# Segment attention with batch norm on one core: batch statistics inside the last attention arm, five output groups loaded into attention's space, output groups in pairs on the two row halves of TensorE

## The chip, the core and the metric

The kernel runs on one NeuronCore of a Trainium2 chip. A core has five engines with an instruction stream each: TensorE (PE, matmuls), VectorE (DVE), ScalarE (ACT), GpSimd (POOL) and SyncE (SP). PE reads SBUF and writes PSUM. DMAs are issued by SP, ACT and POOL, each through a queue of its own, and all share the core's 16 DMA engines. The metric is the device time of one execution in microseconds; the median of 9 runs of the kernel before is 382.57 us (381.2 to 386.01).

## What is computed

`feat` holds 16384 rows of 256 numbers, `bids` a segment number from 0 to 7 for each row. Rows are placed into 8 padded segments of at most 3072 rows, attention runs inside each segment, the result goes through `Wt`, a batch norm over all 16384 rows follows, and its positive part is added to `feat`:

```
q = feat @ Wq; k = feat @ Wk; v = feat @ Wv
starts = jnp.searchsorted(bids, jnp.arange(B, dtype=bids.dtype))
pos = jnp.arange(N, dtype=bids.dtype) - starts[bids]
...
attn = jax.nn.softmax(jnp.where(mask[:, None, :], scores, NEG), axis=-1)
rp = jnp.einsum('blm,bmd->bld', attn, vp)
r = rp[bids, pos]
t = r @ Wt
mu = t.mean(axis=0); var = t.var(axis=0)
tn = (t - mu) / jnp.sqrt(var + EPS) * gamma + beta
return feat + jax.nn.relu(tn)
```

The `bids` of the input are not sorted, so the starts come out as 0, 1441, 1441, 3121, 3677, 3677, 15838 and 15838, and most rows fall outside the padded window of their segment. About 430 to 730 rows per segment have a place of their own ("list" rows); 199 more read a place that another row owns; all others read a row at one end of their segment ("edge" rows, 16 different values in all).

## The kernel before

**Attention.** For each segment `b` a list of at most 6 tiles of 128 rows is gathered by POOL (`gather`, line 821). `project(b)` transposes the tiles on PE (line 904), copies them to `xT` and makes queries, keys (`qs[b % 2]`, `ks[b % 2]`) and values (`vs[b % 2]`, line 938). `scores` (line 948) makes score tiles and ACT's exponentials write them to `pr_a` and `pr_b` (line 953). `sums` (line 983) multiplies them with the values (line 989), divides (lines 993, 994) and leaves the tile in `tk`; `moment` adds it and its square to `acc` (lines 974 to 979). The number of tiles per segment (4, 5 or 6) is known only on the chip, so four segments form one arm of a `tc.Switch` with 81 arms; here the segments take 4, 4, 5, 6 and 6, 6, 4, 4 tiles. Each finished segment is written to `t_rows` in DRAM by SP (line 1005). In the last segment (`b == NB - 1`) POOL gathers the 16 edge rows into `E` (line 1018); `late` and `e_late` add those that lie in the last segment (line 1000); lines 1029 and 1030 finish `E`. Line 1032 takes a square root of a constant on ACT, meant to bring in the square root's table; nothing ties it to this place.

**Between.** Lines 1338 to 1348 check that all denominators are in range and leave a count in `bad`. Then the pools of attention are closed (`att.close()`), and `io` (6 buffers `f` of 1 MB), `fin` and the PSUM pools of the output stage take their space. Lines 1369 to 1388 sum `acc` and `E` over partitions with two matmuls of 512 columns, and make mean, variance, root, `scale` and `shift`; lines 1392 to 1403 turn `E` into the normalised edge rows `y3`, split in three bf16 parts on 48 partitions of each row half of PE.

**Output.** `feat` and `out` are handled as 16 groups of 1024 rows, in the list `ORDER` (0 to 6, 15 to 12, 7 to 11). SP loads a group into one of the 6 buffers (line 1427); for each pair of its 8 row tiles, PE selects the edge rows with the one-hot tile `hot` (line 1435, 48 rows, 256 columns, bf16), and DVE adds the result to the group (line 1446). In four of the steps a second group is taken along, whose `feat` is added on PE through the identity (line 1440, f32) and brought back by ACT (line 1444). ACT issues the group's store (line 1448). Between the groups, `normal` runs the list rows in `tk` through three DVE operations per two tiles (lines 1409, 1412, 1415).

**Scatter.** POOL writes the 48 tiles of `tk` and 3 of `L` to their rows of `out` with one indirect DMA each (`put`, line 1463). The stores of groups and these writes hit the same tensor, so a tile of segment `b` waits until the groups that hold its rows have landed. `waits` gives the number of groups in the order of `ORDER`: for this input 3 for segment 0, 5 for segments 1 and 2, 7 for 3 to 5, 11 for 6 and 7, and all 16 for `L`. The order on DVE and PE after attention is chosen by the scheduler; only the start of the kernel stands in a block with a written order (`tc.manual_schedule`).

Of the kernel before, what the change touches and what calls it, by code (L numbers as in the profile page):

```python
# [9 lines left out]
F32 = mybir.dt.float32  # L10
I32 = mybir.dt.int32
BF16 = mybir.dt.bfloat16
# [6 lines left out]
P = 128  # L19
# [512 lines left out]
def segment_attention_bn_kernel(  # L532
# [43 lines left out]
    with ExitStack() as short:  # L576
# [52 lines left out]
        root = fs.tile([P, 1], F32, name="root")  # L629

# [5 lines left out]
        vs = [fw.tile([P, FT, D + 1], F32, name=f"vs{i}", bufs=1) for i in range(2)]  # L636
        xT = fw.tile([P, DH, FW], F32, name="xT", bufs=1)


        qs = [fw.tile([P, FW], F32, name=f"q{i}", bufs=1) for i in range(2)]  # L640
        ks = [fw.tile([P, 2, P], F32, name=f"k{i}", bufs=1) for i in range(2)]

        pr_a = fw.tile([P, FT, QA], F32, name="pr_a", bufs=1)
        pr_b = fw.tile([P, FT, FW - QA], F32, name="pr_b", bufs=1)
# [338 lines left out]
        def sums(b, u, T, e_late):  # L983
# [13 lines left out]
            if b % PART == PART - 1:  # L997
                moment(at)
            if e_late is not None:
                nc.tensor.matmul(  # L1000
                    e_late, late[:, u, :], tk[:, at, :], start=(u == 0), stop=(u == T - 1)
                )
            if u == TMIN - 1 or u == T - 1:
                u0, u1 = 0 if u < TMIN else TMIN, FT if u == T - 1 else TMIN
                nc.sync.dma_start(
                    t_rows[b * FW + u0 * P : b * FW + u1 * P, :].rearrange(
                        "(t p) d -> p t d", p=P
                    ),
                    tk[:, b * FT + u0 : b * FT + u1, :],
                )  # L1010

        def attend(b, T):
# [15 lines left out]
            if b == NB - 1:  # L1028
                nc.vector.tensor_add(E[:, 0, :], E[:, 0, :], e_late)
                nc.vector.tensor_mul(E[:, 1, :], E[:, 0, :], E[:, 0, :])  # L1030

                nc.scalar.activation(root, eps_t, AF.Sqrt)
# [121 lines left out]
        def edge_selection():  # L1154


            C = N // 2 // (GT * P)
            for c in range(C):
                eb = hotp.tile([P, GT * P], BF16, tag="eb", name=f"eb{c}", bufs=2)
                nc.vector.memset(eb, 99.0)  # L1160
                for r in range(2):
                    nc.sync.dma_start(
                        eb[64 * r : 64 * r + 3 * NE, :],
                        edge_of[ts(r * C + c, GT * P)].unsqueeze(0).to_broadcast(
# [140 lines left out]
        for a in range(NB // PART):  # L1305
# [31 lines left out]

        lim = fw.tile([P, TT], F32, tag="lim", name="lim", bufs=1)
        nc.vector.tensor_scalar(lim, rdens, LIM, None, ALU.is_lt)
        good = fw.tile([P, TT], F32, tag="good", name="good", bufs=1)  # L1340
        odd = fw.tile([P, 1], F32, tag="odd", name="odd", bufs=1)
        nc.vector.scalar_tensor_tensor(
            good, rdens, 1.0 / LIM, lim, ALU.is_gt, ALU.mult, accum_out=odd
        )
        nc.vector.tensor_scalar(odd, odd, -1.0, float(TT), ALU.mult, ALU.add)
        ps_bad = ps_a.tile([P, 1], F32, tag="px", name="ps_bad")
        nc.tensor.matmul(ps_bad, ones, odd, start=True, stop=True)
        nc.vector.tensor_tensor(bad, ps_bad, over, ALU.add)
        att.close()


        fin = short.enter_context(tc.tile_pool(name="fin", bufs=1))
        io = short.enter_context(tc.tile_pool(name="io", bufs=IOB))
        psM = short.enter_context(tc.tile_pool(name="psM", bufs=1, space=PSUM))
        psY = short.enter_context(tc.tile_pool(name="psY", bufs=2, space=PSUM))
        psF = short.enter_context(tc.tile_pool(name="psF", bufs=4, space=PSUM))
        feat3 = feat.rearrange("(g p i) d -> g p i d", p=P, i=GT)
# [11 lines left out]
        sums = psM.tile([P, 2, D], F32, name="sums")  # L1369
        nc.tensor.matmul(sums, ones, acc, start=True, stop=False)  # L1370
        nc.tensor.matmul(sums, wE, E[0:NE, :, :], start=False, stop=True)
        mom = fin.tile([P, 2, D], F32, name="mom")
        nc.vector.tensor_scalar(mom, sums, 1.0 / N, None, ALU.mult)
        mean, var = mom[:, 0, :], mom[:, 1, :]
        sq_m = fin.tile([P, D], F32, name="sq_m")
        nc.vector.tensor_mul(sq_m, mean, mean)
        nc.vector.tensor_sub(var, var, sq_m)
        nc.vector.tensor_scalar(var, var, 0.0, None, ALU.max)
        root_v = fin.tile([P, D], F32, name="root_v")
        nc.scalar.activation(root_v, var, AF.Sqrt, bias=eps_t)  # L1380
        nc.vector.reciprocal(root_v, root_v)
# [4 lines left out]
        nc.vector.tensor_mul(scale[:, 0, :], root_v, gamma_bc)  # L1386
        nc.vector.tensor_mul(shift[:, 0, :], mean, scale[:, 0, :])
        nc.vector.tensor_sub(shift[:, 0, :], beta_bc, shift[:, 0, :])

        yE = fin.tile([P, D], F32, name="yE")
        nc.vector.tensor_mul(yE, E[:, 0, :], scale[:, 0, :])
        nc.vector.tensor_add(yE, yE, shift[:, 0, :])
        nc.vector.tensor_scalar(yE, yE, 0.0, None, ALU.max)
        for s in range(2):
            yh = fin.tile([P, D], BF16, name=f"yh{s}")
            nc.vector.tensor_copy(yh, yE)
            yh_f = fin.tile([P, D], F32, name=f"yhf{s}")
            nc.vector.tensor_scalar(yh_f, yh, later_part[:, s : s + 1], None, ALU.mult)  # L1400
            nc.vector.tensor_sub(yE, yE, yh_f)
        y3 = fin.tile([P, D], BF16, name="y3")
        nc.vector.tensor_copy(y3, yE)  # L1403
        tc.no_sync_barrier()

        def normal(y, x, t, T):

            py = psY.tile([P, 2, D], F32, tag="py", name="py")
            nc.vector.tensor_tensor(
                py[:, 0:T, :], t, scale.to_broadcast([P, T, D]), ALU.mult  # L1410
            )
            nc.vector.tensor_tensor(
                py[:, 0:T, :], py[:, 0:T, :], shift.to_broadcast([P, T, D]), ALU.add
            )
            nc.vector.scalar_tensor_tensor(y, py[:, 0:T, :], 0.0, x, ALU.max, ALU.add)
# [5 lines left out]
        units = iter(range(0, TT, 2))  # L1421
        steps = [(0,), (1,), (2,), (3, 4), (5,), (6, 7), (8,), (9, 10), (11,), (12, 13)]
        for step in [*steps, (14,), (15,)]:
            held = {}
            for k in step:
                held[k] = io.tile([P, GT, D], F32, tag="f", name=f"f{ORDER[k]}")
                nc.sync.dma_start(held[k], feat3[ORDER[k]])
            for i in range(0, GT, 2):
                for k in step:
                    g = ORDER[k]  # L1430
                    r = slice(64 * (g // (NG // 2)), 64 * (g // (NG // 2)) + 3 * NE)
                    pf = psF.tile([P, 2, D], F32, tag="pf", name=f"pf{g}")
                    two, on_pe = held[k][:, i : i + 2, :], k != step[0]
                    for u in range(2):
                        nc.tensor.matmul(  # L1435
                            pf[:, u, :], hot[r, g % (NG // 2), i + u, :], y3[r, :],
                            start=True, stop=not on_pe,
                        )
                        if on_pe:
                            nc.tensor.matmul(  # L1440
                                pf[:, u, :], ident, two[:, u, :], start=False, stop=True
                            )
                    if on_pe:
                        nc.scalar.copy(two, pf)  # L1444
                    else:
                        nc.vector.tensor_add(two, two, pf)  # L1446
            for k in step:
                dense.append(nc.scalar.dma_start(out3[ORDER[k]], held[k]).ins)
# [83 lines left out]
```

## Time and profile before

| what | value |
|---|---|
| median of 9 runs | 382.57 us |
| the profiled execution's own time | 385.01 us |
| its span, first to last instruction | 382.9 us |
| last operation of the last tile in attention (line 1030) | ends at 255.56 us |
| first group load issued | 258.09 us |
| `y3` ready (line 1403) | 273.12 us |
| first store of a group issued | 280.32 us |
| first scatter | 296.25 us |
| last scatter starts | 371.34 us |

Busy shares over the whole span are 75% for PE, 69% for DVE, 45% for POOL and 28% for ACT, but they are averages over very different stages: PE is near full in attention (64.14 of the 66 us from 174 to 240), the DMA engines are nearly idle there (a share of 0.16) and full in the output stage. An entry "L1435 PE MATMUL" means the instruction that line 1435 issued on PE; "PEld" is PE's weight load; "SPq" and "ACTq" are instructions that issue a DMA; the part in brackets is the engine's idle time just before, with what ended it.

### The profile page before, as it was taken

How to read it: one execution, taken by the hardware profiler on the slowest of the kernel's cores; microseconds unless marked ns; L12 is line 12 of the kernel's file. 1: busy time of each engine (PE TensorE's matmuls, PEld its weight loads, DVE VectorE, ACT ScalarE, POOL GpSimd, SP SyncE). 2: the span in 40 equal slices, each digit the busy share in tenths (PEclk: the TensorE clock that was granted, in tenths of full speed). 3: DMA queues.
4: the chain of work that ended last, by engine and by line, in shares of the span. 5: the costliest groups of instructions: out<-in, count | busy, mean ns of one | idle time of the engine just before them, and what ended most of it. 6: DMA issues, size and time to landing. Idle time of an engine off the chain costs nothing. (4 is left out here: it accounts for less than half of the span.)

```text
span 382.9 us, 4089 instructions
## 1 busy us (share of the span) xinstructions
PE 287.3 (75%) x1103; PEld 178.3 (47%) x1103; DVE 263.9 (69%) x789; ACT 105.9 (28%) x199; POOL 173.8 (45%) x180
## 2 busy tenths in 40 slices
PE   1348839879899999599989999953179899897000
PEld 0224626548486578238765777640134443343000
DVE  8988459997959546447992464663996649678930
ACT  8810432222631352354322533411001021111000
POOL 3258377878856766600483000103000537775760
PEclk9999988998999999859999999985555555555555
DMA  4011002031402202111240020239869999999820
GB/s 115 13 34 55 10 8 63 15 113 38 143 19 84 74 22 94 53 43 41 77 139 1 0 85 0 83 103 335 347 239 370 380 373 387 387 417 402 332 81 2
DMA packets 21485, 53.38 MB, mean 139 GB/s; under 512 B 6606, under 2 KB 14112, under 8 KB 17322
## 3 DMA queue, kind: packets, MB, share of 16 engines
q1 hardware_dynamic: 12277, 25.85, 19.5%
q10 hardware_dynamic: 2421, 16.83, 10.6%
q0 software_dynamic: 6720, 10.02, 8.4%
q14 instruction: 51, 0.42, 0.4%
q8 instruction: 16, 0.26, 0.3%
HBM read 26.67 MB, written 29.92 MB: 148 GB/s over the span
## 5 line engine op out<-in xcount | busy, mean ns | idle before, releaser
L821 POOL DMA_INDIRECT xs<-in_r_feat,idx x48 | 58.8, 1225 | 61.0 <-DVE upto L871 43.1
L989 PE MATMUL po<-vs,pr_a 128*128 128x257 f32 x312 | 77.2, 391 | 4.5 <-ACT pr_a L953 2.9
L1463 POOL DMA_INDIRECT out<-tk,idx x48 | 47.3, 985 | 57.9 <-DMA f<-in_r_feat 33.0
L989 PEld LDWEIGHTS po<-vs,pr_a 128*128 128x128 f32 x312 | 57.3, 193 | 18.5 <-ACT pr_a L953 5.0
L821 POOL DMA_INDIRECT reads_r<-reads_of,idx x48 | 51.2, 1067 | 21.7 <-issue 12.5
L1435 PE MATMUL pf<-y,hot 48*128 48x256 bf16 x128 | 36.5, 399 | 22.3 <-DVE y L1403 11.1
L1446 DVE TENSOR_TENSOR f<-f,pf 128x512 f32<-128x512 f32 x48 | 30.9, 686 | 18.3 <-PE pf L1435 18.2
L934 PE MATMUL pv<-wvt,xT 128*128 128x256 f32 x164 | 39.2, 393 | 0.0
L1435 PEld LDWEIGHTS <-hot 48*128 48x128 bf16 x128 | 14.2, 122 | 51.9 <-issue 48.2
L1440 PE MATMUL pf<-f,ident 128*128 128x256 f32 x64 | 37.9, 706 | 0.0
L934 PEld LDWEIGHTS pv<-wvt,xT 128*128 128x128 f32 x164 | 31.9, 198 | 9.1 <-ACT q L926 2.0
L948 PE MATMUL s<-q,k 32*128 32x512 f32 (+2 forms) x124 | 31.8, 566 | 3.0 <-DVE q L925 3.0
L978 ACT ACTIVATE sq<-tk 128x256 f32<-128x256 f32 x39 | 16.3, 417 | 62.7 <-DVE tk L994 51.7
L1444 ACT COPY f<-pf 128x512 f32<-128x512 f32 x16 | 9.4, 586 | 73.7 <-PE pf L1440 73.7
L904 PE MATMUL px<-ident,xs 128*128 128x128 f32 x82 | 17.6, 329 | 15.8 <-DVE xT L908 5.6
L953 ACT ACTIVATE pr_a<-s,mask 128x512 f32<-128x512 f32 x39 | 24.1, 687 | 18.1 <-PE s L948 17.9
L915 PE MATMUL pqk<-xT,wqk 128*128 128x512 f32 (+2 forms) x52 | 25.1, 629 | 0.3 <-DVE xT L908 0.3
L904 PEld LDWEIGHTS px<-ident,xs 128*128 128x128 f32 x82 | 10.3, 160 | 28.4 <-issue 13.0
L1440 PEld LDWEIGHTS pf<-f,ident 128*128 128x128 f32 x64 | 16.5, 312 | 11.2 <-issue 10.7
L993 DVE RECIPROCAL rdens<-po 128x1 f32<-128x1 f32 x39 | 6.3, 163 | 21.7 <-PE po L989 21.6
L938 ACT COPY vs<-pv 128x512 f32<-128x512 f32 (+1 forms) x21 | 12.1, 577 | 30.4 <-PE pv L934 30.4
L821 POOL DMA_INDIRECT E<-t_rows,eidx x1 | 1.1, 1074 | 42.8 <-issue 42.8
(241 smaller groups left out, 414.3 us busy)
## 6 DMA issues: line engine op xcount, KB each, us to landing
f<-in_r_feat SPq DMA_DIRECT2D x16, 1024.0 KB, 8.6
out<-f ACTq DMA_DIRECT2D x16, 1024.0 KB, 8.8
t_rows<-tk SPq DMA_DIRECT2D x4, 768.0 KB, 3.9
t_rows<-tk SPq DMA_DIRECT2D x4, 512.0 KB, 3.2
eb<-edge_of SPq DMA_DIRECT2D x16, 96.0 KB, 2.4
t_rows<-tk SPq DMA_DIRECT2D x4, 256.0 KB, 2.4
xs<-in_r_feat,idx POOLq DMA_INDIRECT x48, 2.8
reads_r<-reads_of,idx POOLq DMA_INDIRECT x48, 2.5
```

What stands on the lines that cost most here:

```text
L821: nc.gpsimd.indirect_dma_start(out=dst, out_offset=None, in_=table, in_offset=bass.IndirectOffsetOnAxis(ap=ind, axis=0), bounds_check=n - ...
L904: nc.tensor.transpose(px[:, ts(t, P)], xs[:, b * FT + t0 + t, ts(h, P)], ident)
L915: nc.tensor.matmul(pqk[:, 0:w], wqk[:, h, :], xT[:, h, own_c], start=(h == 0), stop=(h == DH - 1),)
L934: nc.tensor.matmul(pv[:, t, :], xT[:, h, ts(t0 + t, P)], wvt[:, h, :], start=(h == 0), stop=(h == DH - 1),)
L948: nc.tensor.matmul(s[:, i, 0:w], k[g, t // 4, :], q[g, c : c + w], start=True, stop=True)
L953: nc.scalar.activation((pr_b if c else pr_a)[:, t, 0:w], s[:, i, 0:w], AF.Exp, bias=mask[:, m : m + 1],)
L978: nc.scalar.activation(sq, tk[:, at, :], AF.Square)
L989: nc.tensor.matmul(po, pr[:, t, ts(r, P)], v[:, t, :], start=(t == 0), stop=(t == T - 1))
L1435: nc.tensor.matmul(pf[:, u, :], hot[r, g % (NG // 2), i + u, :], y3[r, :], start=True, stop=not on_pe,)
L1440: nc.tensor.matmul(pf[:, u, :], ident, two[:, u, :], start=False, stop=True)
L1446: nc.vector.tensor_add(two, two, pf)
L1463: w = nc.gpsimd.indirect_dma_start(out=out, out_offset=bass.IndirectOffsetOnAxis(ap=idx[:, at : at + 1], axis=0), in_=y, in_offset=None, b ...
```

## The change

The diff below leaves out comments, the parts that only move, and the last arm's unchanged lines.

- `xT`, `qs`, `ks`, `vs`, `pr_a` and `pr_b` become slices of one tile `work` that lives as long as the kernel's main part. Five group buffers (`f_bufs`) are other views of the same space; a sixth is made in `io` after attention. Buffer 0 covers `xT` and part of the even queries, buffer 1 the rest of the queries, the keys and part of the even values, buffers 2 to 4 the rest, with all of `pr_a` and most of `pr_b`.
- At the end of the last segment's `attend`, SP issues the loads of the first five groups, and `statistics()` makes mean, root, `scale_s` and `y3` there, on tiles that exist already (`late` as scratch). In the instruction order of the arm that this input takes, SP issues the load of buffer 0 before the store of segment 6 to `t_rows`, and the other four after it.
- Line 1032's square root is replaced by one on the denominator of the last tile but one, so it cannot run earlier. In the instruction order this removes two table loads from the arm's first segment and puts one between the squares of the last segment's tiles.
- The store of the last segment to `t_rows` goes from SP to POOL.
- Groups go in pairs of consecutive entries of `ORDER`. Each pair has an even and an odd group, and `hot` keeps even groups in one row half and odd ones in the other, so PE gets alternating halves. Pairs 0 and 1 add both groups on DVE; pairs 2 to 7 add the even entry on DVE and the odd one on PE and ACT. Operations of the list rows follow each add: none in pairs 0 and 1, 4 in pairs 2 and 3, then 3. The order on DVE and PE is the written one.
- `short_path_holds` (the check of the denominators) comes after pair 3. `scale` and `shift` are made after pair 1.
- `L` waits for the largest count among the segments (11 here) instead of 16. The bound of the scatter's index check is put in a register once.

```
+        wide = DH * FW + 2 * FW + 4 * P + 2 * FT * (D + 1) + FT * FW
+        work = fs.tile([P, wide], F32, name="work")
...
+        parts = [work[:, c : c + n] for c, n in zip(begins, sizes)]
+        xT = parts[0].rearrange("p (h c) -> p h c", h=DH)
+        qs = parts[1:3]
...
+        f_bufs = [
+            work[:, c : c + GT * D].rearrange("p (i d) -> p i d", i=GT)
+            for c in range(0, sum(sizes) - GT * D + 1, GT * D)
+        ]
...
+            if b == NB - 1 and u == T - 2:
+                nc.scalar.activation(root, rdens[:, one], AF.Sqrt)
...
+                dma = nc.sync if b < NB - 1 else nc.gpsimd
+                dma.dma_start(
...
+        def statistics():
+            free = late.rearrange("p t m -> p (t m)")
+            msq, var, yE = (free[:, ts(i, D)] for i in range(3))
+            s1 = ps_o.tile([P, D], F32, tag="po", name="s1")
+            s2 = ps_o.tile([P, D], F32, tag="po", name="s2")
+            for i, ps in enumerate((s1, s2)):
+                nc.tensor.matmul(ps, ones, acc[:, i, :], start=True, stop=False)
+            for i, ps in enumerate((s1, s2)):
+                nc.tensor.matmul(ps, wE, E[0:NE, i, :], start=False, stop=True)
+            nc.vector.tensor_scalar(mean, s1, 1.0 / N, None, ALU.mult)
+            nc.vector.tensor_mul(msq, mean, mean)
+            nc.vector.scalar_tensor_tensor(var, s2, 1.0 / N, msq, ALU.mult, ALU.subtract)
+            nc.vector.tensor_scalar(var, var, 0.0, None, ALU.max)
+            nc.scalar.activation(msq, var, AF.Sqrt, bias=eps_t)
+            nc.vector.tensor_sub(yE, E[:, 0, :], mean)
+            nc.vector.reciprocal(var, msq)
+            nc.vector.tensor_mul(scale_s, var, gamma_bc)
+            nc.vector.tensor_mul(yE, yE, scale_s)
+            nc.vector.tensor_add(yE, yE, beta_bc)
+            later = [later_part[:, s : s + 1] for s in range(2)]
+            nc.vector.tensor_scalar(y_part, yE, 0.0, later[0], ALU.max, ALU.mult)
+            nc.vector.scalar_tensor_tensor(yE, yE, 0.0, y_part, ALU.max, ALU.subtract)
+            nc.vector.tensor_scalar(y_part, yE, later[1], None, ALU.mult)
+            nc.vector.tensor_sub(y3, yE, y_part)
...
-                nc.scalar.activation(root, eps_t, AF.Sqrt)
+                for g, f in zip(ORDER, f_bufs):
+                    nc.sync.dma_start(f, feat3[g])
+                statistics()
...
-                        edge_of[ts(r * C + c, GT * P)].unsqueeze(0).to_broadcast(
+                        edge_of[ts(2 * c + r, GT * P)].unsqueeze(0).to_broadcast(
...
-        psF = short.enter_context(tc.tile_pool(name="psF", bufs=4, space=PSUM))
+        psF = short.enter_context(tc.tile_pool(name="psF", bufs=5, space=PSUM))
...
-        steps = [(0,), (1,), (2,), (3, 4), (5,), (6, 7), (8,), (9, 10), (11,), (12, 13)]
+        pairs = [(k, k + 1) for k in range(0, NG, 2)]
+        n_ops = [0, 0, 4, 4, 3, 3, 3, 3]
+        with tc.manual_schedule(engines={mybir.EngineType.DVE, mybir.EngineType.PE}):
+            for n, pair in enumerate(pairs):
+                for k in pair:
+                    if k >= len(ahead):
+                        nc.sync.dma_start(f_bufs[k % IOB], feat3[ORDER[k]])
+                for i in range(0, GT, 2):
+                    pfs = {}
+                    for k in pair:
+                        pfs[k] = psF.tile([P, 2, D], F32, tag="pf", name=f"pf{ORDER[k]}")
+                    for u in range(2):
+                        for k in pair:
+                            half, c = ORDER[k] % 2, ORDER[k] // 2
+                            r = slice(64 * half, 64 * half + 3 * NE)
+                            on_pe = n > 1 and k % 2
+                            nc.tensor.matmul(
+                                pfs[k][:, u, :], hot[r, c, i + u, :], y3[r, :],
+                                start=True, stop=not on_pe,
+                            )
+                        if on_pe:
+                            nc.tensor.matmul(
+                                pfs[k][:, u, :], ident, f_bufs[k % IOB][:, i + u, :],
+                                start=False, stop=True,
+                            )
+                    for k in pair:
+                        two = f_bufs[k % IOB][:, i : i + 2, :]
+                        if n > 1 and k % 2:
+                            nc.scalar.copy(two, pfs[k])
+                        else:
+                            nc.vector.tensor_add(two, two, pfs[k])
+                    for _ in range(n_ops[n]):
+                        next(row, None)
+                for k in pair:
+                    dense.append(nc.scalar.dma_start(out3[ORDER[k]], f_bufs[k % IOB]).ins)
+                if n == 1:
+                    nc.vector.tensor_copy(scale[:, 0, :], scale_s)
+                    nc.vector.tensor_mul(shift[:, 0, :], mean, scale[:, 0, :])
+                    nc.vector.tensor_sub(shift[:, 0, :], beta_bc, shift[:, 0, :])
+                if n == 3:
+                    short_path_holds()
...
-                put(L[:, t, :], TT + t, NG)
+                put(L[:, t, :], TT + t, max(waits.values()))
```

`row` steps through the three operations of `normal`, for two tiles at a time, one operation per `next`. In the instruction order of the changed kernel ACT keeps its own, not written, order: the store of the even group of pair 2 stands behind ACT's first copy of pair 3, that of pair 5 behind the first two copies of pair 6, and that of pair 6 behind the first two copies of pair 7.

## The prediction

> **What bounds the kernel now.** I read the busy times by stage first (columns: stretch, its us, then busy us and instructions of PE, PEld, DVE, ACT and POOL, granted PE clock, DMA share, GB/s).
>
> ```profile
> 258.00:274.00 16.00, 4.70 (x8) 1.46 (x9) 9.24 (x21) 1.79 (x2) 2.98 (x3) 0.50 0.92 358
> 274.00:280.00 6.00, 2.65 (x12) 1.35 (x11) 6.00 (x11) 0.00 (x0) 0.00 (x0) 0.50 0.34 139
> 280.00:290.00 10.00, 7.80 (x26) 2.98 (x24) 9.86 (x17) 0.00 (x0) 0.00 (x0) 0.50 0.89 301
> 290.00:360.00 70.00, 59.36 (x156) 25.95 (x155) 51.82 (x87) 9.38 (x16) 40.99 (x42) 0.50 1.00 391
> 360.00:374.00 14.00, 0.00 (x0) 0.00 (x0) 6.72 (x13) 0.00 (x0) 9.25 (x10) 0.50 0.37 134
> ```
>
> From 290 to 360 the DMA engines are full at 391 GB/s, with PE at half clock and 85% busy. From 274 to 280 they idle: all six buffers are full and no group is finished. Next, the timeline of what the first group waits for.
>
> ```profile
> 255.14 0.42 DVE L1030 TENSOR_TENSOR E<-E 128x256 f32<-128x256 f32 x1
> ...
> 262.32 0.69 DVE L1373 TENSOR_SCALAR mom<-sums 128x512 f32<-128x512 f32 x1 [4.22 <-PE sums L1371]
> ...
> 264.48 1.28 ACT L1380 ACT_TABLE_LOAD   x1 [10.22 <-DVE mom L1378]
> 265.77 0.51 ACT L1380 ACTIVATE root_v<-mom,eps_t 128x256 f32<-128x256 f32 x1
> 266.31 1.75 DVE L1381 RECIPROCAL root_v<-root_v 128x256 f32<-128x256 f32 x1 [2.06 <-ACT root_v L1380]
> ...
> 272.83 0.29 DVE L1403 CAST y<-yE 128x256 bf16<-128x256 f32 x1
> ...
> 277.81 4.87 DVE L1446 TENSOR_TENSOR f<-f,pf 128x512 f32<-128x512 f32 x8
> ```
>
> The edge rows take 17.6 us after attention, and list rows hold DVE 4.7 us more before the first add (277.81). Last, POOL's waits and the end of its timeline:
>
> ```profile
> POOL out L1463 <- DMA f<-in_r_feat: 33.0, 1, 33.0
> POOL out L1463 <- DMA out<-f: 5.6, 1, 5.6
> ```
> ```profile
> 371.34 0.99 POOL L1463 DMA_INDIRECT out<-L,idx  x1 [0.30 <-issue]
> ```
>
> 51 scatters at 1.29 us (0.99 + 0.30) are 65.8 us; the chain starts at 296.25, when the third stored group has landed, and loses 10.4 in waits. The last one starts at 371.34, lands 2.1 later (smallest landing of that tensor), and the span ends at 382.95, 9.5 after that. So two chains set the end: POOL's, and the DMA traffic behind it. Both begin with the edge rows.
>
> **1. Attention.** Two table loads leave ACT at 164 to 169. There PE runs a score matmul from 164.73 to 166.8 and ACT waits 5.6 for PE afterwards, so I take 0 (gain up to 1.5 = 1.28 + 0.20). The new table load stands between squares, where ACT idles 1.93 a time: 0, at most 1.28.
>
> **2. Loads.** Buffer 0 is free when the last values are made (238.2), buffer 1 after the last first scores (243.1), 2 to 4 after the last product (253.0), 5 after the last square (254.8); before, the first load went at 258.09. At 386 GB/s (the row 260 to 270) one takes 2.7, so with the 0.8 MB of `t_rows` behind the same engines buffer 4 lands near 265 and 5 near 268. Pairs 0 and 1 need buffers 0 to 3 at 266 (some 4 us of cover), pair 2 needs 4 and 5 at 278. On SP's queue load 0 goes ahead of segment 6's store, but that waits for its tile until 242.85 anyway. Load 1 shares the engines with this store: the gather of `E` (247.45, landing 2.7 later) can slip 2.7, to 252.9, and is needed at 254.69; without this 1.8 of cover `y3` slips one for one. The last store on POOL's queue has only three gathers of `L` and the scatters of 285 behind it; `L` is needed near 350. Cost 0.
>
> **3. Edge rows.** The check leaves the path (255.70 to 258.10). Matmuls of 512 columns took 2.07 each; the four of 256 are 1.04 each, the `acc` pair can start at 254.8, so the second sum is there at 258.9. Then mean 0.40, square 0.43, difference 0.42, variance 0.48, clamp 0.29 (from 258.0: 260.2 with gaps of 0.04), root 0.51 + 0.25 (table there already), reciprocal 1.75, and seven operations of 0.35 to 0.48 (2.86) with 0.3 of gaps: `y3` at 265.9, 7.2 earlier. Bounds: 264.8 if PE keeps its full clock through the sums, 268 if the gather of `E` is late.
>
> **4. Pairs 0 and 1.** First add at 266.8 (0.25 to the first matmul, 0.6 for two). 16 adds at 0.61 (4.87/8): groups 0 and 1 stored at 271.2 and 271.8, before 280.32; the third at 276.2, before 285.71. `scale` and `shift` 1.2: 277.8.
>
> **5. Pairs 2 to 7.** PE first: one step is a selection for each half and an identity matmul.
>
> ```profile
> 307.38 0.39 PE L1435 MATMUL pf<-y,hot 48*128 48x256 bf16 x1
> 307.70 1.22 PE L1440 MATMUL pf<-f,ident 128*128 128x256 f32 x2
> 308.85 0.39 PE L1435 MATMUL pf<-y,hot 48*128 48x256 bf16 x1
> ```
> ```profile
> 311.80 0.60 PE L1435 MATMUL pf<-y,hot 48*128 48x256 bf16 x3
> ```
> ```profile
> 320.89 0.82 PE L1435 MATMUL pf<-y,hot 48*128 48x256 bf16 x3
> ```
>
> A step with one selection lasts 1.475. Three selections took 0.60 in the step whose groups lie in both halves (6 and 15), and 0.82 where all three lie in one: the other half's is hidden. So a step stays between 1.475 and 1.775 (one in series: 4.76/16 = 0.30); I take 1.475, 8 per pair = 11.8. DVE: pairs 2 and 3 have 5 operations per two tiles, 20 x 0.62 = 12.4; later pairs 9.9. Pairs 2 and 3 thus go by DVE, to 302.6. The check costs 0.55 on DVE (0.19 + 0.21 + 0.15, lines 1339 to 1345) and 0.7 of PE (0.58 and the hand-over), and PE's next pair stands behind it: PE restarts at 303.9. Four pairs by PE: 351.1, last copy 351.7. A pair moves 4.2 MB plus about 0.6 MB of scatter, 409 GB/s at this pace against 391 had: transfers queue. Group transfers landed after 4.3 to 14.0 us, median 8.7. With 14.0 for both store 8 (316.3) and load 14, pair 7, due at 339.3, starts 5.0 late; with the median 0. I take 5.0: 356.7. Last stores land at 8.7: 365.4; with 9.5 behind, 374.9.
>
> The Trainium skill, "TensorEngine Tiling (Array Packing)", section "Key Properties", speaks against this step: it says that changing the tiling mode, not just the tile, drains the engine, and each step goes from 64-row tiles to the whole array and back. The row 307.38 to 308.85 holds one such round trip already, 0.32 from selection to identity. By the trace the sum stays; if a second selection made the drain 0.11 longer (0.32 less 0.21, my estimate from three selections, 0.82 less 0.60), 48 steps would give 5.3 us more.
>
> **6. POOL.** First scatter at 276.2 + 10.3 (as before, 285.71 to 296.0) = 286.5. The seventh waits for group 4, whose store stands behind ACT's first copy of pair 3 (near 293.7) and lands 8.8 later: 302.5, a wait of 8. Twelve go to 318; group 6 (stored at 302.6) has landed. Eighteen to 341.2. Group 10's store stands behind two copies of pair 6: 334, landed 342.8. 14 more starts: 360.9; with the two issue gaps of before (1.84 and 3.05), 365.8 at most; then 2.1 + 9.5: 372.5 to 377.4, the middle 375. The bounds register takes away one MOVE of 29 ns per scatter, at most 1.5 in all and off DMA issue: 0. `L` at 11 groups instead of 16: 0, since it comes last and late.
>
> **Sum.** Both chains end near 375 on the trace's clock, against 382.95: 7.9 less. The profiled execution took 385.01, 2.4 above the median; I take the difference from the median, 382.57: 374.7, rounded to 375.
>
> **Rivals.**
> A, the forecast: 375, own range 370 to 380. Chance 0.62.
> B, DMA is the only wall. For: share 1.00 at 391 for 70 us; PE and DVE pass it if loads are never late and PE's clock rises. The stages above moved 38.8 MB; less six loads and `L` (6.7), 32.1 MB remain at 271.2: 82.1 us, 353.3, and 2.1 + 9.5 behind: 364.9, so 364.5. Against: POOL's chain alone needs 286.5 + 65.8 + 9.5 = 361.8 with no wait at all, and two waits are seen. 0.14.
> C, POOL's chain gives the start back. If groups 4, 6 and 10 land in 14.0 and DVE's row operations or the check bring group 10's store to 341, fifteen scatters start at 355: the last at 373.1, end 384.7 less the two issue gaps, if those fall into waits: 379.8 to 384.7, as a time 382. Against: before, most groups landed in 8.7. 0.12.
> D, slower: PE becomes the bound. If halves don't overlap while an identity matmul stands between them, and the switch costs 0.11 more, a step is 1.885: 277.8 + 48 x 1.885 + 1.3 + 0.6 + 8.7 + 9.5 = 388.4, so 388. It is slower from 1.81 per step on; 1.775 (no overlap alone) gives 382.7. Against: the row at 311.80; for: two more groups are added on PE (48 identity matmuls, not 32). 0.12.
> That the early loads don't start early (the slices of `work` tied to one another) costs little, since pairs 0 and 1 find them by 266 even from 253: inside A.
>
> **How the numbers follow.** A change of 0.5%, 1.9 us, is about what a measurement can tell. A (but for 0.02) and B are faster, C's lower part too (0.03): 0.77. Same: 0.02 of A, 0.08 of C, 0.03 of D: 0.13. Slower: 0.10. The range 366 to 382.5 leaves out B's lowest part and most of D.
>
> **What would show it.** `y3` near 266 and the first store near 271; group loads at 238 and 243; a step near 1.475 in pairs 4 to 7 and two selections starting together; the seventh scatter waiting about 8 us. Wrong if a step exceeds 1.8, if a load is late by more than 8, or if `E` comes after 254.7.

## The result and the profile after

The changed kernel takes 376.34 us, the median of 20 runs (374.69 to 378.87). The kernel before took 384.10 us, the median of 62 runs (378.07 to 389.5), beside it. The ratio is 0.9871, 95% interval 0.9849 to 0.9892. The profiled execution of the changed kernel took 376.05 us, with a span of 373.9. Ratios here and below leave out disturbed runs of both kernels, so 0.9871 is not the quotient of the two medians (0.980), and where one kernel's times fall into two groups, both groups are told.

First the stages of the changed kernel (columns as in the first view of the prediction: stretch, its us, then busy us and instructions of PE, PEld, DVE, ACT and POOL, granted PE clock, DMA share, GB/s).

```profile
258.00:274.00 16.00, 9.72 (x40) 3.18 (x40) 14.92 (x27) 0.00 (x0) 3.04 (x3) 0.50 0.84 328
274.00:280.00 6.00, 6.00 (x17) 2.42 (x16) 5.88 (x10) 1.17 (x2) 0.00 (x0) 0.50 0.99 384
280.00:290.00 10.00, 6.13 (x19) 2.53 (x18) 8.22 (x13) 1.17 (x2) 4.36 (x5) 0.50 1.00 376
290.00:350.00 60.00, 54.97 (x148) 22.30 (x147) 49.97 (x82) 10.58 (x19) 37.43 (x39) 0.50 0.93 357
350.00:374.00 24.00, 2.88 (x8) 1.10 (x6) 1.89 (x5) 1.13 (x2) 8.46 (x9) 0.50 0.33 121
```

The hole from 274 to 280 (DMA share 0.34 before) is gone: 0.99 now. The transfers end sooner too: from 340 to 350 their share is 0.66.

Next, the timeline of the way from attention to the first group, in the changed kernel.

```profile
253.33 1.18 PE L1044 MATMUL s<-acc,ones 128*128 128x256 f32 x4
253.61 0.42 DVE L1080 TENSOR_TENSOR E<-E,e_late 128x256 f32<-128x256 f32 x1
254.06 0.42 DVE L1081 TENSOR_TENSOR E<-E 128x256 f32<-128x256 f32 x1
...
254.44 1.13 PE L1046 MATMUL s<-E,wE 16*128 16x256 f32 x4
255.17 0.42 DVE L1047 TENSOR_SCALAR mean<-s 128x256 f32<-128x256 f32 x1 [0.69 <-PE s L1046]
...
257.15 0.51 ACT L1051 ACTIVATE late<-late,eps_t 128x256 f32<-128x256 f32 x1 [3.97 <-DVE late L1050]
257.69 1.75 DVE L1053 RECIPROCAL late<-late 128x256 f32<-128x256 f32 x1 [0.63 <-ACT late L1051]
...
262.09 0.43 DVE L1061 TENSOR_TENSOR y<-late,y_part 128x256 bf16<-128x256 f32 x1
...
263.28 1.88 DVE L1484 TENSOR_TENSOR work<-work,pf 128x512 f32<-128x512 f32 x3 [0.77 <-PE pf L1470]
```

`E` is finished at 254.48 (255.56 before) and the edge rows `y3` at 262.52 (273.12): 8.03 us after `E` where it was 17.56. Of the 9.5 us saved, 6.1 lie between `E` and the mean (0.69 now; 262.32 - 255.56 = 6.76 before, with the check and sums at half clock), 1.5 between the mean and the root (1.98 now, 3.45 before, the table load among them) and 2.0 between the reciprocal and `y3` (3.08 now, 5.06 before). The half clock of before stands in its own rows: the granted clock from 257 to 262.5 is 0.50, and the sums took 2.08 and 2.07 where they take 1.18 and 1.13 now (1.00 from 253 to 256).

```profile
257.31 0.58 PE L1347 MATMUL ps_bad<-odd,ones 128*128 128x1 f32 x2 [2.82 <-DVE odd L1345]
258.15 2.08 PE L1370 MATMUL sums<-acc,ones 128*128 128x512 f32 x2 [0.25 <-DVE bad L1348]
260.15 2.07 PE L1371 MATMUL sums<-E,wE 16*128 16x512 f32 x2
```

Last, what PE and POOL wait for in the output stage of the changed kernel (PE's waits, then POOL's own line of the timeline). From here on groups are counted along `ORDER` from 0, as in the prediction's steps 5 and 6; pair 3 holds groups 6 and 7.

```profile
PE ps_bad L1427 <- DVE odd L1425: 4.0, 1, 4.0
PE pf L1475 <- DMA work<-in_r_feat: 3.9, 1, 3.9
```
```profile
283.67 1.02 POOL L1503 DMA_INDIRECT out<-tk,idx  x1 [12.37 <-DVE py L1443]
...
299.96 0.98 POOL L1503 DMA_INDIRECT out<-tk,idx  x1 [8.04 <-DVE py L1443]
...
341.87 0.98 POOL L1503 DMA_INDIRECT out<-tk,idx  x1 [3.55 <-DVE py L1443]
```

PE stops twice for some 4 us: for the load of group 7 in pair 3, and for the check behind pair 3. POOL's first scatter starts at 283.67 (296.25 before); its two later waits end when groups 4 and 10 have landed (299.11 and 341.07), though the view names DVE, whose operations were long done. The last stores are issued at 353.53 and 353.99 and land by 362.84. The last scatter starts at 359.91 and lands at 363.77, 3.9 after its start where it was 2.1 before, and the span ends 10.1 us after that (9.5 before).

Runs differ in when attention ends. So the profiled executions, those of the experiments too, are compared from the end of `E` on; this table is worked out from their timelines (us after `E`, except for the first column).

| kernel | `E` done | `y3` | first add | first scatter | last scatter | last copy or add of a group | end |
|---|---|---|---|---|---|---|---|
| before | 255.56 | 17.56 | 22.25 | 40.7 | 115.8 | 104.8 | 127.4 |
| changed | 254.48 | 8.03 | 8.80 | 29.2 | 105.4 | 99.0 | 119.4 |
| changed, again | 258.15 | 8.03 | 9.20 | 29.4 | 106.1 | 100.3 | 120.4 |
| statistics alone | 256.38 | 8.03 | 8.86 | 33.3 | 108.0 | 97.0 | 119.4 |
| loads after | 255.11 | 8.03 | 8.79 | 26.9 | 105.3 | 98.0 | 118.5 |
| statistics after | 259.97 | 15.73 | 16.50 | 36.5 | 111.7 | 104.8 | 124.6 |
| both after | 258.77 | 8.66 | 9.42 | 27.5 | 103.0 | 97.7 | 118.0 |
| edge rows after | 256.64 | 7.90 | 8.67 | 29.5 | 103.6 | 97.8 | 117.7 |
| old halves | 255.19 | 8.03 | 9.01 | 29.3 | 105.7 | 103.5 | 123.3 |
| check early, ACT in order | 259.77 | 8.03 | 8.80 | 27.8 | 101.1 | 94.8 | 114.3 |

From `y3` to the end it is 109.8 before and 111.4 after. So 9.5 us were won ahead of `y3`, and 1.6 of them were lost behind it. They were lost at the very end: from `y3` to the start of the last scatter it is 98.2 before and 97.4 after, and from there to the end 11.6 before and 14.0 after.

### The profile page after: what moved, and what is told of

Its sections match the earlier page's. It is cut to its first block, busy times and chain, and to the rows that moved or that the text cites. A ratio compares the mean times of both kernels' runs of the same rounds, so it can differ in the third digit from the quotient of the medians.

```text
span 373.9 us, 4126 instructions
## 1 busy us (share of the span) xinstructions
PE 292.5 (78%) x1139; PEld 177.7 (48%) x1139; DVE 263.0 (70%) x779; ACT 108.1 (29%) x205; POOL 173.4 (46%) x181
## 5 line engine op out<-in xcount | busy, mean ns | idle before, releaser
L1007 PE MATMUL po<-work 128*128 128x257 f32 x394 | 95.5, 389 | 4.0 <-ACT work L971 2.3
L1007 PEld LDWEIGHTS po<-work 128*128 128x128 f32 x394 | 73.0, 193 | 21.0 <-issue 5.4
L1475 PE MATMUL pf<-work,ident 128*128 128x256 f32 x64 | 39.1, 714 | 3.9 <-DMA work<-in_r_feat 3.9
L971 ACT ACTIVATE work<-s,mask 128x512 f32<-128x512 f32 (+2 forms) x62 | 32.4, 599 | 24.7 <-PE s L966 24.4
L952 PE MATMUL pv<-wvt,work 128*128 128x256 f32 x164 | 37.8, 383 | 0.0
L966 PE MATMUL s<-work 32*128 32x512 f32 (+2 forms) x124 | 32.5, 562 | 3.2 <-DVE work L943 3.2
L952 PEld LDWEIGHTS pv<-wvt,work 128*128 128x128 f32 x164 | 30.7, 190 | 8.3 <-ACT work L944 1.8
L1484 DVE TENSOR_TENSOR work<-work,pf 128x512 f32<-128x512 f32 x40 | 26.1, 684 | 11.7 <-PE pf L1470 11.7
L933 PE MATMUL pqk<-work,wqk 128*128 128x512 f32 (+2 forms) x52 | 24.2, 609 | 0.3 <-DVE work L926 0.3
L1475 PEld LDWEIGHTS pf<-work,ident 128*128 128x128 f32 x64 | 16.0, 310 | 13.2 <-issue 9.1
```

The lines of the kernel that those rows point to most:

```text
L933: nc.tensor.matmul(pqk[:, 0:w], wqk[:, h, :], xT[:, h, own_c], start=(h == 0), stop=(h == DH - 1),)
L952: nc.tensor.matmul(pv[:, t, :], xT[:, h, ts(t0 + t, P)], wvt[:, h, :], start=(h == 0), stop=(h == DH - 1),)
L966: nc.tensor.matmul(s[:, i, 0:w], k[g, t // 4, :], q[g, c : c + w], start=True, stop=True)
L971: nc.scalar.activation((pr_b if c else pr_a)[:, t, 0:w], s[:, i, 0:w], AF.Exp, bias=mask[:, m : m + 1],)
L1007: nc.tensor.matmul(po, pr[:, t, ts(r, P)], v[:, t, :], start=(t == 0), stop=(t == T - 1))
L1475: nc.tensor.matmul(pfs[k][:, u, :], ident, f_bufs[k % IOB][:, i + u, :], start=False, stop=True,)
```

## The experiments

Four kernels ran beside the kernel before at 383.20 us (23 runs).

**Loads after the arms.**

```
-                for g, f in zip(ORDER, f_bufs):
-                    nc.sync.dma_start(f, feat3[g])
                 statistics()
...
         ahead = list(f_bufs)
+        for g, f in zip(ORDER, ahead):
+            nc.sync.dma_start(f, feat3[g])
```

> The first five groups are loaded after the arms (near 258) and no longer inside the last one; all else as in the changed kernel. Theory 'start' (the edge rows are ready 10.6 earlier and this comes through to the end; the early loads only serve it): five loads of 2.7 us follow each other from 258, so the first add moves from 263.3 to 264 to 267 and pairs 1 and 2 still find their groups; 0 to +3 us on 376.3. Rival 'loads' (5 MB taken out of the full stretch of DMA made the gain): 5 x 2.7 us come back, less what idle engines between 258 and 268 take, +6 or more, that is 382 or more.

Measured: 377.52 us (375.67 to 378.18), ratio 0.9882 (0.984 to 0.9925). The time is in the range of the theory "start", but the edit did not do what was meant. SP leaves the arm early, since the last segment's store is on POOL, so the five loads were issued at 246.6 to 253.1 and not at 258 (237.2 to 252.4 in the changed kernel). What loads from 258 on cost is told by the kernel with the statistics alone, below.

**Statistics after the arms.**

```
                     nc.sync.dma_start(f, feat3[g])
-                statistics()
...
+        statistics()
         att.close()
```

> The statistics and edge rows are computed after the arms instead of inside the last one, with the same operations; the early loads stay. Theory 'start': the sums begin near 257 at half clock (4 x 1.04), and the 6.9 us from the last sum to the edge rows stay, so these come near 268 instead of 262.5; the end follows by 4 to 6 us: 380 to 382. Rival 'loads': 0 to +1, 377. Rival 'DMA wall': between 0 and +3, since the stretch with DMA full starts later but is shorter.

Measured: 385.14 us; one run took 375.78, the other five 384.33 to 386.40. The five lie above every theory; the one lies within the changed kernel's own range, near where the rivals "loads" and "DMA wall" had it. The profile is of the run with 386.40; here is its timeline around the end of the arm.

```profile
258.20 0.70 PE L1021 MATMUL e_late<-tk,late 128*128 128x256 f32 x2 [0.78 <-DVE tk L1012]
...
259.55 0.42 DVE L1081 TENSOR_TENSOR E<-E 128x256 f32<-128x256 f32 x1
...
265.13 2.04 PE L1044 MATMUL s<-acc,ones 128*128 128x256 f32 x4 [6.23 <-issue]
267.10 2.07 PE L1046 MATMUL s<-E,wE 16*128 16x256 f32 x4
```

The data for the first sum are there by 259.2, yet PE starts it at 265.13. "issue" means that PE waited for nothing that the profile shows. The jump out of the arm fills this stretch: in the trace PE's branch instruction lasts from 258.20 to 264.89. The clock has fallen to half meanwhile (granted 0.50 from 265 on; 2.04 for what took 1.18 in the arm).

**Both after the arms.** The two edits together.

> Both edits together: loads and statistics after the arms, so that only the new output stage is left of the change. Theory 'start': as with the statistics alone, since the loads have landed by 268 even from 258: 380 to 383, near the kernel before. Rival 'output stage' (the pairs on two row halves and the written order made the gain): at most 378.

Measured: 384.34 us, 12 runs from 376.58 to 387.48, nine of them at 383.15 or more; the ratio, 0.9907 (0.9829 to 0.9986), is that of the other three. The profile is of a run with 378.93.

```profile
257.59 1.10 PE L1044 MATMUL s<-acc,ones 128*128 128x256 f32 x4 [1.06 <-DVE acc L997]
...
258.63 1.12 PE L1046 MATMUL s<-E,wE 16*128 16x256 f32 x4
```

In this run PE's branch instruction lasted 1.60 (255.83 to 257.43), PE waited 1.06 and kept its clock, and `y3` came 8.66 after `E`, where the other kernel's run had 15.73. The 7.1 us between them are about the 6.6 between their ends (124.6 and 118.0). So in a run in which PE resumes at once a place after the arms costs 0.6 at `y3` (ACT's root starts 0.8 after its data) and nothing that is seen at the end; in a run in which PE resumes late it costs some 7 us. For the same reason the short times don't speak for the rival "output stage": they kept the early start. That the other long times of these two kernels have the same cause is argued, not shown: there is no trace of them. It fits that PE's jump took about 7 us in most of the traces of this case (last section).

**Old halves.** The groups of most pairs lie on the same half again.

```
-                        edge_of[ts(2 * c + r, GT * P)].unsqueeze(0).to_broadcast(
+                        edge_of[ts(r * C + c, GT * P)].unsqueeze(0).to_broadcast(
...
-                            half, c = ORDER[k] % 2, ORDER[k] // 2
+                            half, c = ORDER[k] // (NG // 2), ORDER[k] % (NG // 2)
```

> The groups 0 to 7 lie on one row half and 8 to 15 on the other, as before the change; all else as in the changed kernel. The pairs (0,1), (2,3), (4,5), (14,13), (8,9), (10,11) then have both selections in one half. Theory 'PE sets the pace from 303 on': a step of these pairs rises from 1.475 to 1.69 to 1.78, three of the last four pairs are 8 steps each: +5 to +7 us on the last copy, and 1 more for pair 2: 381 to 384. Rival 'DMA wall' (engines at share 1.00 and PE only follows them): 0 to +2. Rival 'halves do not overlap': no difference in the step and 0.

Measured: 380.88 us (379.09 to 383.27), ratio 0.9961 (0.9929 to 0.9993), against 0.9871 for the changed kernel. PE's timeline in pair 4, with the old halves first, then in the changed kernel:

```profile
304.18 0.61 PE L1470 MATMUL pf<-y,hot 48*128 48x256 bf16 x2
304.72 1.22 PE L1475 MATMUL pf<-work,ident 128*128 128x256 f32 x2
305.87 0.60 PE L1470 MATMUL pf<-y,hot 48*128 48x256 bf16 x2
```
```profile
303.32 0.39 PE L1470 MATMUL pf<-y,hot 48*128 48x256 bf16 x2
303.64 1.22 PE L1475 MATMUL pf<-work,ident 128*128 128x256 f32 x2
304.80 0.40 PE L1470 MATMUL pf<-y,hot 48*128 48x256 bf16 x2
```

Two selections take 0.60 in one half and 0.39 to 0.40 in two. The step is 1.69 (305.87 - 304.18) instead of 1.48, at the lower edge of what was expected; the last copy comes 4.5 later after `E` and the end 3.9. PE's pace does set the end, a little more weakly than the 5 to 7 expected, and "DMA wall" (0 to +2) is out. The last scatter starts only 0.3 later after `E`, but lands 7.1 after its start instead of 3.9: the last stores, issued later, are still under way then.

Four more kernels ran on a chip on which everything took longer: the kernel before 411.67 us (399.16 to 416.05, 11 runs).

**Check early; ACT in order; both; both with a seventh buffer.** The first edit, and the second:

```
             nc.vector.tensor_scalar(odd, odd, -1.0, float(TT), ALU.mult, ALU.add)
+            yield
             ps_bad = psF.tile([P, 1], F32, tag="pf", name="ps_bad")
...
-                if n == 3:
-                    short_path_holds()
+                if n in (2, 3):
+                    next(check, None)
```
```
-        with tc.manual_schedule(engines={mybir.EngineType.DVE, mybir.EngineType.PE}):
+        with tc.manual_schedule(
+            engines={mybir.EngineType.DVE, mybir.EngineType.PE, mybir.EngineType.Activation}
+        ):
```

The fourth kernel has besides:

```
-IOB = 6
+IOB = 7
...
-        shift = fin.tile([P, 1, D], F32, name="shift")
+        shift = mean.unsqueeze(1)
```

> The three DVE operations of the check on the denominators go behind pair 2, its matmul and its last operation stay behind pair 3: nothing is left out. Theory 'PE's pace sets the end together with POOL's chain': PE no longer waits 4.0 for DVE there and DVE not 0.7 and 1.6 for PE; the last copy moves from 353.5 to near 350, the scatter that waits 3.55 for group 10 no longer waits: -3 to -3.5, 373. Rival 'DMA wall': 0 to -1.

> ACT's instructions of the output stage keep the written order too, so each pair's two stores go ahead of the next pair's copies. The store of group 4 moves from 290.1 to near 285 and the seventh scatter from 300 to near 295. Theory 'the later wait takes it over' (PE's pace decides when group 10 is stored): the wait of 3.55 for group 10 grows by the 5 us, the end stays: -0.5 to +0.5. Rival 'POOL's chain alone sets the end': -3 to -5. Rival 'ACT now waits in stores for DVE and holds PE's copies': +1 or more.

> Both edits: the check's DVE part behind pair 2, and ACT in the written order. By the theory of PE's pace no more than the check alone, since group 10 is stored when PE has come to it: 373. If POOL's chain were the tighter one, 370 or less.

> Both edits and a seventh buffer of group size (the shift is kept in the mean's place), so that group 6 is loaded before any store and group 7 takes the first buffer that comes free. Theory: PE's wait of 3.9 for the load at pair 3 goes, DVE then sets pairs 2 and 3 (274.1 + 2 x 12.4 = 298.9), PE starts pair 4 near 297 instead of 303.3: -5 to -6 against the changed kernel, 370 to 371. Rival 'DMA wall': no better than the kernel with both edits alone. Rival 'one more load ahead delays the first stores': the first scatter later than 283.7 and the end with it, 374.

Measured: medians of 407.19, 401.80, 400.53 and 403.02 us; ratios 1.0179 (1.0078 to 1.028), 1.0087 (0.9983 to 1.0192), 0.9993 (0.9874 to 1.0112) and 1.0085 (1.0049 to 1.0122). By the medians alone all four are below the kernel before (0.973 to 0.989), so not even the sign is clear. The changed kernel did not run there. The profiles hold long stops that no wait on the kernel's own engines explains, for instance two of the first kernel: ACT stands 12.20 ("remote") up to 75.92, and PE 7.45 ("issue") up to 348.27.

The first lies in attention, which the edits don't touch; `E` was done at 275 to 284 in the four. These runs say nothing about the edits. The seventh buffer and each edit alone stay open.

The last four ran beside the kernel before at 384.12 us (11 runs).

**The changed kernel again.**

> The changed kernel itself, as a yardstick beside these three: 0.987 of the kernel before, as measured.

Measured: 377.36 us (375.57 to 380.30), ratio 0.9843 (0.9795 to 0.9892): the yardstick holds.

**The statistics alone.** The kernel before gets `statistics()` and the root between the squares, and loses what they replace; in the output stage:

```
+            if step == (1,):
+                tc.no_sync_barrier()
+                nc.vector.tensor_copy(scale[:, 0, :], scale_s)
+                nc.vector.tensor_mul(shift[:, 0, :], mean, scale[:, 0, :])
+                nc.vector.tensor_sub(shift[:, 0, :], beta_bc, shift[:, 0, :])
+            if step == (6, 7):
+                short_path_holds()
             n_rows = 0 if step[0] < 2 else (3 if len(step) == 2 else 2)
```

> The kernel before with the new statistics alone: statistics and edge rows in the last arm, the root's table load between the squares, the check behind the groups 6 and 7; loads (all from 258), steps, buffers and order of the output stage as before, save that scale and shift follow group 1. Theory 'the shorter way from attention to the edge rows made the gain': edge rows at 263 to 266, first add near 265 instead of 277.8, and the old output stage keeps its pace: 373 to 378, that is 0.975 to 0.99 of before, as the whole change. Rival 'it takes the early loads and the pairs to use the earlier start' (three loads come after the first add and the old steps do not follow): 0.993 or more of before.

Measured: 377.81 us (375.93 to 381.28), ratio 0.9863 (0.9805 to 0.9922), beside 0.9843 for the whole change: the same within the noise. By the table the two agree up to the first add (8.86 and 8.80) and at the end (119.4 both). The first loads go out at 259.0 here, and the first add still comes when `y3` is there. What the rest of the change moves in between cancels. POOL's last scatter starts 2.6 sooner in the changed kernel (105.4 against 108.0 after `E`), but the last copy comes 2.0 later (99.0 against 97.0). With the statistics alone the last store has landed 8.4 ahead of the last scatter, which lands 2.1 after its start with the end 9.2 behind it; in the changed kernel the two landings are 0.9 apart, and these pieces are 3.9 and 10.1. Which parts of the new statistics (the check, the sums' place, the table load, the fewer DVE operations) bring how much on the clock was not tried one by one.

**Edge rows after the arms.** The sums, the variance and the root stay in the arm, the nine DVE operations behind them leave it.

```
             nc.scalar.activation(msq, var, AF.Sqrt, bias=eps_t)
+
+        def edge_rows():
+            free = late.rearrange("p t m -> p (t m)")
+            msq, var, yE = (free[:, ts(i, D)] for i in range(3))
             nc.vector.tensor_sub(yE, E[:, 0, :], mean)
...
+        edge_rows()
         att.close()
```

> The changed kernel with its statistics cut in two: sums, variance and root stay in the last arm, the nine DVE operations from the reciprocal to the edge rows come after the arms. Theory 'the place matters only through the jump out of the arm' (an engine took 0.6 on DVE, but 5.2 on ACT, 5.6 on SP and 5.2 on PE, in the run with the statistics after the arms, until its next instruction): PE, ACT and SP jump while DVE works, DVE's jump of 0.6 is all that is added: +0.5 to +1 against the changed kernel, and no times 8 above. Rival 'leaving the arm before the edge rows costs what the statistics after the arms cost': +6 to +9.

Measured: 377.74 us (376.40 to 383.10), ratio 0.9871 (0.9812 to 0.993); 0.4 above the yardstick, with one time of six 5.4 above the median. `y3` comes 7.90 after `E`, and DVE loses 0.27 at the jump (the 5.2 that the expectation gives for PE is 6.7 by its branch record):

```profile
259.35 0.43 DVE L1057 TENSOR_TENSOR late<-E,mean 128x256 f32<-128x256 f32 x1 [0.27 <-issue]
259.71 1.75 DVE L1058 RECIPROCAL late<-late 128x256 f32<-128x256 f32 x1
```

So what DVE does may lie on either side of the jump; what matters is that PE's sums are ahead of it, and less so ACT's root, which was not tried alone (0.8 in the profile with both after the arms).

**Check early and ACT in order, beside the changed kernel.**

> The kernel with the check's DVE part behind pair 2 and ACT in the written order, a second time, beside the changed kernel itself. Theory of PE's pace: 0.99 of the changed kernel (-3 to -3.5). Rival 'DMA wall': 0.997 to 1.

Measured: 375.83 us (374.34 to 377.71), ratio 0.9805 (0.9756 to 0.9855), against 0.9843 (0.9795 to 0.9892): 1.5 us better by the medians (0.996 of the changed kernel), with intervals that overlap, so a gain on the clock is not shown; the rival's 0.997 to 1 is nearer than the theory's 0.99. In the profile the edits do what they should:

```profile
302.62 1.22 PE L1479 MATMUL pf<-work,ident 128*128 128x256 f32 x2
303.63 0.42 PE L1428 MATMUL ps_bad<-odd,ones 128*128 128x1 f32 x2
303.99 0.89 PE L1474 MATMUL pf<-y,hot 48*128 48x256 bf16 x2
```

PE goes through the check without a stop, the seventh scatter waits 4.91 instead of 8.04, and from `E` to the end it is 114.3, 5.1 to 6.1 less than in the two profiles of the changed kernel. But `E` was done at 259.77 in this run, against 254.48 and 258.15, in code that is the same up to there. Whether later starts belong to this kernel or to chance can't be told from three profiles.

## Why the prediction was right, step by step

**Attention, 0.** The two profiles of the changed kernel end it at 254.48 and 258.15, one before and one after the 255.56 of the kernel before. A gain of the 0 to 1.5 that was allowed for can't be seen in that.

**Loads, 0.** They went out at 237.2, 242.3, 250.5, 252.0, 252.4 and 258.6, close to the times worked out but for the sixth, which was due at 254.8 and waited for SP's jump; `E` was not late for it. What the step didn't say is that early loads have no worth of their own here: with loads from 259 the first add comes just as soon.

**Edge rows at 265.9.** Measured 262.5, ahead even of the lower bound of 264.8; 1.1 of the 3.4 come from attention, which ended at 254.48 in this profile, and counted from `E` it is 8.03 instead of 10.3. The way was right and one term too large: four matmuls at half clock behind `E` were to bring the second sum at 258.9, but PE came straight from attention with its clock at full speed, four pieces took 1.13 to 1.18, and the mean began 0.69 after `E`. The run with the statistics after the arms shows the other case: 2.04 to 2.07, at half clock.

**Pairs 0 to 3.** 16 adds took 9.66 (9.8 was worked out). Pairs 2 and 3 went by DVE, as said, but took 13.1 and 13.0 where 12.4 was worked out. The late load was expected at pair 7 with 5.0; none came there, and one came at pair 3 with 3.9 for PE and 1.6 for DVE. The buffer that decided was the second one to be used again: its load took 11.6, within the 4.3 to 14.0 that the prediction had, but used for pair 7 alone. That the two waits are of like size is chance. The check cost PE a stop of 4.0, because PE had come to it early and stood behind DVE's whole queue of list rows; from the end of these rows to PE's restart it is 1.5, where 1.3 was worked out. From 274.1 to PE's restart it is 29.2, not 26.1.

**Pairs 4 to 7.** A step of 1.48, as the row said (1.475). From PE's restart to the last copy's end it is 50.2; 47.8 was worked out, and 52.8 with the late load that did not come. The Trainium skill, "TensorEngine Tiling (Array Packing)", section "Key Properties", was weighed for a longer drain when the tiling mode changes. No run shows one: from the selections to the identity matmul it is 0.32, with one selection before the change and with two after. The same section says that different tiles work independently; 0.39 for two selections in two halves and 0.60 in one agree with it.

**POOL.** The first scatter came at 283.67 (286.5 worked out), the seventh waited 8.04 (8), and the wait for group 10 was there. The last start, 359.91, is 1.0 under the 360.9 to 365.8: group 10's store had landed 1.7 sooner than worked out (341.07), with 0.8 from there to the scatter, and the two gaps with "issue" of the kernel before (1.84 and 3.05), which make the upper end, did not come back. The kernel with the statistics alone has them (1.84 and 5.19); the changed kernel and its variants of the first and last four, whose scatters have no MOVE of the bound, have no such gap above 1.4. That the MOVE is the reason was not tried.

**The sum.** 374.9 on the trace's clock was worked out, and 373.9 came; as a time 375, and 376.34. Part of that is luck, since errors of both signs cancel. The start was 3.4 earlier than worked out, and the 5.0 for the load at pair 7 was not needed; against that, pairs 2 and 3 lost 3.1 more, the last scatter landed 3.9 after its start instead of 2.1, and the end came 10.1 instead of 9.5 after that. The two chains did end together, as forecast: the last store landed at 362.84, the last scatter at 363.77. That the stores' traffic delays this scatter fits the old halves (7.1), but was not tried alone. The first add came 13.45 sooner after `E`, the end 8.0: 4.7 of the difference are list rows that were moved behind the first add, where the sum has them too.

**The rivals.** B (DMA the only wall, 364.5) is out: the longer step of the old halves shows at the end, and the DMA engines are no longer full from 340 on. C (POOL gives the start back) is out: counted from `E`, the first scatter is 11.5 sooner and the last 10.4. D (halves don't overlap) is out; without two halves it would have cost 3.9 in the profile and 0.9% on the clock.

## What to carry to other kernels

Before a whole stage is rebuilt, shorten the serial chain in front of it: here the shorter way to the edge rows alone gives the whole gain that could be measured, and loads, pairs and order moved time from one chain to the other. Put what PE and ACT must do for such a chain ahead of a jump out of a branch, and let the engine that resumes soonest work across it. Compare profiles from a common event near the change, since the time up to there can differ by more than the change brings.

## What the runs showed of the hardware

**Jumps out of a branch.** From the trace's branch records, an engine's time from its last jump out of the arm to its next instruction was 0.6 on DVE, 5.2 on ACT and 5.6 on SP in the changed kernel, where group loads were in flight; before, with no loads yet, it was 3.1 on ACT and 3.6 on SP. On SP this holds in all 14 profiles: 3.6 to 3.7 in the four without group loads in flight, 5.1 to 6.9 in the others. PE's branch instruction lasted 6.7 to 8.0 in nine profiles, 3.5 in the kernel before and 0.4 to 1.6 in four; what decides is open, since loads were in flight in both sorts. The statistics in the arm hide this, which the prediction did not have among its reasons: in the changed kernel PE's jump took from 254.54 to 261.57, just within the way to `y3`. In the profile of the kernel before it cost about 1.0 (the check's last operand was ready at 256.33, PE began it at 257.31).

**PE's clock.** Here are 20 us of the changed kernel's output stage:

```profile
310.00:330.00 20.00, 20.00 (x56) 7.97 (x55) 17.42 (x28) 3.51 (x6) 15.16 (x16) 0.50 1.00 378
```

PE is busy for 20.00 of 20 us and the granted clock stays at 0.50. The Trainium skill, "TensorE: Matmul & The Clock Gate", section "Part 1: The HAM clock gate (the "warmup" mystery)", says that a few microseconds of sustained work lift it to full speed. In this stage that does not happen, and the measurement decides. In the old output stage, with the statistics alone, the clock did rise: it was 1.00 from 286 to 290, after 6 us with PE busy all the time, and back at 0.50 from 293.

**The same code at other speeds.** On one chip the kernel before took 411.67 us where others gave 383.20 and 384.12, and the profiles of four kernels there hold stops of 7 to 12 us that no wait on their own engines explains. Among the kernels on one other chip, attention, the same in all, ended between 255.11 and 259.97.
